# Self-attention on one Trainium2 core: projections and output product on unpadded heads, moved to and from 32-row places through DRAM, and a branch that waits for the mask alone

## The chip, the cores and the metric

The kernel runs on one core of one Trainium2 chip. The metric is the device time of one execution in microseconds (us), given as the median of several runs. A profile is one execution recorded by the hardware. Its engines are TensorE (PE; its weight loads are PEld), VectorE (DVE), ScalarE (ACT), GpSimd (POOL) and SyncE (SP). Each takes its instructions from a queue of its own, in order. SyncE, ScalarE and GpSimd also issue DMAs from their queues; when a DMA has landed, it raises a semaphore, and an instruction that needs the data waits for it on its own engine's queue.

## The reference, cut to what matters

The input x is 8 x 512 x 256 (batches, places, channels), with a side input for attention biases, a condition and a mask of padded places. Two residual steps follow each other, each of two blocks:

```python
x = x + attn(cond(x, bias, mask, cond_64))   # masked attention with a null key, then attention over the heads of a place
x = x + ffn(cond2(x, cond_64))               # a mixture of 8 experts (two per token) and shared ones, then the layer below
```

`ffn` is a transformer layer, and its self-attention is what most of the change touches:

```python
qkv = x @ wi.T + bi
q, k, v = jnp.split(qkv, 3, axis=-1)          # 16 heads of 16 channels each
scores = jnp.einsum('bhqd,bhkd->bhqk', q, k) / jnp.sqrt(hd)
attn = jax.nn.softmax(scores, axis=-1)
o = jnp.einsum('bhqk,bhkd->bhqd', attn, v)
x = layernorm(x + o @ wo.T + bo)
x = layernorm(x + hier_moe(x))                # 8 experts, one per token
```

Only where a key of the mask allows it does `cond` attend to that key; a key is kept where the mask is true, and queries see keys up to their own place and the null key.

## The kernel before, in words

Everything is 32-bit float. P = 128 partitions, S = 512 places in NT = 4 tiles, D = 256 channels in KD = 2 halves, B = 8 batches, H = 16 heads of HD = 16 channels.

**Head and branch.** For this mask no key among the first 384 places is kept in any batch. The kernel tests that: two loads of the mask to one partition, two reductions (L363 to L368), and a value read into registers (L1111) for a branch (L1112) that every engine takes. `any_keys` handles the general case and does not run here; `late_keys` (L812) runs, and attends only from the last 128 queries. Ahead of the branch stand, in queue order, the loads of the constants, of the first attention's weights (wq and wo of 1 MB each, wkv; L370 to L388), of the over-heads attention's weights (`load_oh`, L218), and products with the null key on VectorE (L398, L404). The experts' router and shared weights (L1232 and after) are loaded once the branch is taken.

**Order of the work.** The kernel is one long program, written as Python generators that are advanced by hand. The order in which their calls are recorded, rearranged a little by a scheduler, is the order of each engine's queue. `late_keys` runs together with the routing of the first batches (`route`, `mixture`). From about 388 to 1560 us the self-attention runs in a loop of 256 half steps j, over 32 groups n = j // 8, each of 4 heads of a batch (4 groups a batch). Beside it a plan of side work (routing, experts' matmuls, the next batches' beginnings) is advanced so that it is done by given half steps (`goals`). From 1560 us the last mixture runs.

**Padded heads.** TensorE takes a head's 16 channels as rows that begin at a multiple of 32. So before the change each head has 32 rows, of which 16 hold channels: the projection weights wqp, wkp and the output weights wop are read padded (256 x 512 and 512 x 256), 4 heads fill 128 rows, and the row behind a head's channels holds a one in k and, in q, the negative maximum of a query's scores, so that the second score product gives scores less their maximum.

**One half step** (`half(j)`, h = j % 8) issues, in this order:
- `both` (L1643): two heads' first scores (pss, L1616) for a group ten half steps ahead (8 + LEAD), each reduced to its negative maximum on VectorE (nmz, L1618), and two heads' second scores (pst, L1640) of this group, each passed through exp on ScalarE (pT_s, L1641). pss and pst share four PSUM banks.
- at h = 6, `augment` (L1626): maxima transposed (pm) and added into q_s.
- at h = 1 and 2, `project(n + 2)` (L1561): pq_s (L1568; 4 matmul records a group) evicted by VectorE with bias and scale (L1570), then pk_s (L1574) evicted by ScalarE (L1576). The results q_s and k_s are used where they lie.
- at h = 2 to 5, a step of `divide` (L1676) of the group before; at the end of a batch, `end` (L1696) of the batch before, from the sixth half on.
- side work, and at h = 2, 4, 6 and 7 `gather` (po_s, L1663), four heads' products of weights and values over one tile of keys. v has a column of ones, so that the row behind a head's 16 output rows holds its sums.

**Quotient and output product.** `divide` copies po_s to oT_s on ScalarE (L1679), sends the four rows of sums over 128 partitions (8 KB DMA on ScalarE's queue, L1685), takes reciprocals (L1687), sends them back as rows (SyncE, L1688), and two halves later spreads them over the heads' rows with one product by the constant selb (prs, L1692) and multiplies (L1693). `end` multiplies with wop: four matmuls a tile, one for each padded group (px_s, L1703).

Outside the change, but used as a row to compare with: the experts' result leaves through a 256 KB store from ScalarE's queue (`y<-y`, L1453; 48 times).

Of the kernel before, what the change touches and what calls it, by code (L numbers as in the profile page):

```python
# [9 lines left out]
F32 = mybir.dt.float32  # L10
# [11 lines left out]
H = 16  # L22
# [18 lines left out]
def tile_adaln_attn_ffn(ctx: ExitStack, tc: tile.TileContext, a: dict, out: bass.AP):  # L41
# [29 lines left out]
    cst = keep.tile([P, 270], F32, name="cst", tag="cst")  # L71
    nc.sync.dma_start(cst, a["c_misc"])
    selb = cst[:, 0:128]
    rank8, rank4, rank2 = cst[:, 256:264], cst[:, 264:268], cst[:, 268:270]
# [39 lines left out]
    with nc.allow_non_contiguous_dma(reason="narrow rows"):  # L114
        nc.sync.dma_start(w_chosen, a["w_route"].rearrange("(k p) n -> p k n", p=P))
    br_bc = mid.tile([P, 12], F32, name="br_bc", tag="br_bc")
    nc.scalar.dma_start(br_bc, rows_of(a["b_route"]))
# [77 lines left out]
    none = ohp.tile([P, places // P], I32, name="none", tag="prod", bufs=4)  # L195
    nc.gpsimd.memset(none, B * S)
    nc.sync.dma_start(ids_d.rearrange("(p n) o -> p (n o)", p=P), none)
# [8 lines left out]
    def oh_load(name, shape, src, eng=None):  # L206
        t = ohp.tile(shape, F32, name=name, tag=name)
        (eng or nc.sync).dma_start(t, src)
        return t

    def oh_wload(name, src, cols):
        n = src.shape[0] // P
        return oh_load(name, [P, n, cols], src.rearrange("(k p) n -> p k n", p=P))

    OH_STEPS = 29
    oh_w = {}

    def load_oh():  # L218
        with nc.allow_non_contiguous_dma(reason="small vectors by partition"):
            oh_w["gout"] = oh_load("gout", [P, KD], cols_of(a["g_out"]), nc.scalar)  # L220
            oh_w["bdown"] = oh_load("bdown", [64, 1], a["bdown"].unsqueeze(1), nc.scalar)
        oh_w["awq"] = oh_wload("awq", a["aWq"], D)
        oh_w["awd"] = oh_wload("awd", a["aWdown"], 64)
        oh_w["awup"] = oh_load("awup", [64, 512], a["aWup"])
        oh_w["awout"] = oh_wload("awout", a["aWout"], D)
        oh_w["bq"] = oh_load("bq_bc", [P, D], rows_of(a["bq"]), nc.scalar)
        oh_w["bup"] = oh_load("bup_bc", [P, 2 * D], rows_of(a["bup"]), nc.scalar)
        oh_w["bout"] = oh_load("bout_bc", [P, D], rows_of(a["bout"]), nc.scalar)
# [134 lines left out]
    kept_i = aw.tile([1, 3], I32, name="kept", tag="kept")  # L363
    for u in range(2):
        early_keys = ohp.tile([1, B // 2, LAST * P], U8, name="early_keys", tag="prod", bufs=4)
        nc.sync.dma_start(early_keys, a["mask"][u * (B // 2) : (u + 1) * (B // 2), 0 : LAST * P].unsqueeze(0))
        nc.vector.tensor_reduce(kept_i[:, u : u + 1], early_keys, AX.XY, ALU.max)
    nc.vector.tensor_tensor(kept_i[:, 2:3], kept_i[:, 0:1], kept_i[:, 1:2], ALU.max)  # L368

    def load(name, shape, src, eng=None):  # L370
        t = aw.tile(shape, F32, name=name, tag=name)
        (eng or nc.sync).dma_start(t, src)
        return t

    def wload(name, src, cols):
        n = src.shape[0] // P
        return load(name, [P, n, cols], src.rearrange("(k p) n -> p k n", p=P))

    with nc.allow_non_contiguous_dma(reason="small vectors by partition"):
        gin = load("gin", [P, KD], cols_of(a["g_in"]), nc.scalar)  # L380
        nvcol = aw.tile([P, 1], F32, name="nvcol", tag="nvcol")
        for j in range(2):
            nc.scalar.dma_start(nvcol[j * 64 : (j + 1) * 64, :], a["cond"][1].unsqueeze(1))
    wq = wload("wq", a["Wq"], H * DH)
    wo = wload("wo", a["Wo"], D)
    wkv = wload("wkv", a["Wkv"], 2 * DH)
    nk_bc = load("nk_bc", [P, DH], rows_of(a["cond"][0]), nc.scalar)
    nv_bc = load("nv_bc", [P, DH], rows_of(a["cond"][1]), nc.scalar)  # L388
    nb_bc = load("nb_bc", [P, H], rows_of(a["null_bias"]), nc.scalar)
    load_oh()  # L390
    bias_v = a["attn_bias"].rearrange("(g hh j) q k -> g j q hh k", g=2, hh=4, j=2)


    wn = aw.tile([P, KD, 2, 2, 4], F32, name="wn", tag="wn")
    for k in range(KD):
        for g in range(2):
            pr = ohp.tile([P, 8, DH], F32, name="wn_pr", tag="prod", bufs=4)
            nc.vector.tensor_tensor(  # L398
                pr,
                wq[:, k, g * 512 : (g + 1) * 512].rearrange("p (h d) -> p h d", h=8),  # L400
                bc(nk_bc, 1, 8),
                ALU.mult,
            )
            nc.vector.tensor_reduce(  # L404
                wn[:, k, g].rearrange("p j hh -> p hh j"),
                pr.rearrange("p (hh j) d -> p hh j d", j=2),
                AX.X,
                ALU.add,
            )
# [8 lines left out]
    def any_keys():  # L418
        fill()
# [392 lines left out]
    def late_keys(first_group):  # L812
# [3 lines left out]
        with ExitStack() as ph:  # L816
# [14 lines left out]
            load_x(0)  # L831
            load_x(1)
# [5 lines left out]
            for g in range(2):  # L838
                for j in range(2):
                    nc.sync.dma_start(bias[:, g, j], bias_v[g, j, tail, :, tail])  # L840
                    nc.gpsimd.affine_select(
                        out=bias[:, g, j],
                        in_=bias[:, g, j],
                        pattern=[[0, 4], [-1, P]],
                        compare_op=ALU.is_ge,
                        fill=MASKED,
                        base=0,
                        channel_multiplier=1,
                    )
            ones = wp.tile([1, P], F32, name="ones", tag="ones")  # L850
# [6 lines left out]


            nvb = wp.tile([P, P], F32, name="nvb", tag="nvb")
            nc.vector.tensor_copy(nvb, nvcol.to_broadcast([P, P]))  # L860
            pn = ps_m.tile([P, D], F32, name="pn", tag="m")
            for c in range(8):
                nc.tensor.matmul(pn, nvb, wo[:, c, :], start=(c == 0), stop=(c == 7))
            null_row = wp.tile([1, D], F32, name="null_row", tag="null_row")
            nc.scalar.copy(null_row, pn[0:1, :])
            mv, rs = ln_stats(wk, [pn])
            row = wp.tile([P, D], F32, name="row", tag="row")
            nc.vector.tensor_scalar(row, pn, mv[:, 0, 0:1], rs[:, 0:1], ALU.subtract, ALU.mult)
# [212 lines left out]
            for _ in range(6):  # L1081
                next(prep)

# [27 lines left out]
    kept = nc.values_load(kept_i[:, 2:3], min_val=0, max_val=1)  # L1111
# [110 lines left out]
    with ExitStack() as ph:  # L1222
# [16 lines left out]
        with nc.allow_non_contiguous_dma(reason="small vectors by partition"):  # L1239
            wtT = wload("wtT", a["wtT"], E)  # L1240
            wgT = load("wgT", [64, E], a["wgT"], nc.scalar)
            gT = load("gT", [64, B], a["condT"], nc.scalar)
        swg = wload("swg", a["sw_gate"], 2 * P)
        swu = wload("swu", a["sw_up"], 2 * P)
        swd = wload("swd", a["sw_down"], D)
# [266 lines left out]
        late_keys(chain(route(0), route(1), mixture(0), mixed(0)))  # L1512
# [7 lines left out]
        with nc.allow_non_contiguous_dma(reason="small vectors by partition"):  # L1520
            bqp = load("bqp", [P, 4], cols_of(a["bq_pad"]), nc.scalar)
            bkp = load("bkp", [P, 4], cols_of(a["bk_pad"]), nc.scalar)
        wqp = wload("wqp", a["wq_pad"], 512)
        wkp = wload("wkp", a["wk_pad"], 512)
        wv = wp.tile([P, KD, H, HD], F32, name="wv", tag="wv")
        bv_bc = wp.tile([P, H, HD], F32, name="bv_bc", tag="bv_bc")
        with nc.allow_non_contiguous_dma(reason="values without their padding"):
            for k in range(KD):
                nc.sync.dma_start(
                    wv[:, k], a["wv_pad"][k * P : (k + 1) * P, :].rearrange("p (h d) -> p h d", h=H)[:, :, 0:HD]  # L1530
                )
# [3 lines left out]
        wop = wload("wop", a["wo_pad"], D)  # L1535
# [4 lines left out]
        for t_ in v_sets:  # L1540
# [7 lines left out]
        kone = wp.tile([P, 1], F32, name="kone", tag="kone")  # L1548
        nc.vector.tensor_reduce(
            kone, selb.rearrange("p (h r) -> p h r", h=4)[:, :, 0], AX.X, ALU.add  # L1550
        )
        nc.vector.tensor_tensor(bkp, bkp, kone.to_broadcast([P, 4]), ALU.add)
# [8 lines left out]
        def project(n):  # L1561

            b, g = divmod(n, 4)
# [3 lines left out]
            for k in range(KD):  # L1567
                nc.tensor.matmul(pq, wqp[:, k, gs], yT[:, k, :], start=(k == 0), stop=(k == KD - 1))  # L1568
            q = qs[n] = wk.tile([P, S], F32, name="q_s", tag="q_s", bufs=3)
            nc.vector.tensor_scalar(q, pq, bqp[:, g : g + 1], HD**-0.5, ALU.add, ALU.mult)  # L1570
            yield
            pk = ps_m.tile([P, S], F32, name="pk_s", tag="m")
            for k in range(KD):
                nc.tensor.matmul(pk, wkp[:, k, gs], yT[:, k, :], start=(k == 0), stop=(k == KD - 1))  # L1574
# [498 lines left out]
```

## Time and profile before

| what | value |
|---|---|
| median of 6 runs | 1818.4 us (1815.45 to 1832.13) |
| profiled execution | 1812.23 us |
| its span | 1810.4 us |
| mean granted TensorE clock | 0.902 |
| instructions in the span | 23,454 |
| loop, 405 to 1560 us: TensorE, VectorE, ScalarE, GpSimd busy | 1062.1, 662.5, 411.2, 253.3 us |
| loop: mean share of the DMA engines | 0.23 |

In the profile's busy line an engine's name is followed by its busy time, its share of the span and its number of instructions. A group's row gives the line, the engine, the operation, output and inputs with partitions x elements, and the count; then busy time and mean ns of one; then the idle time just before those instructions, with what ended most of it (`<-DVE nmz L1618` means that VectorE's work at line 1618 ended the wait). A row of the timeline gives start and length in us, then the engine, the line and the operation, with the idle time before it in brackets. The chain is the work that ended last, followed back from the end of the span: each share is what an engine or line holds of it. "DMA share" is the mean busy share of the core's 16 DMA engines. The granted clock is TensorE's, as a fraction of full speed.

The loop's DMA traffic is uneven: from 565 to 660, 860 to 960 and 1165 to 1250 us, where experts' weights stream in, the share is 0.54, 0.67 and 0.61; from 1300 to 1420 us it is 0.03.

### The profile page before, as it was taken

What the parts mean: (1) busy time and instruction counts of PE and PEld (TensorE: products, weight loads), DVE (VectorE), ACT (ScalarE), POOL (GpSimd) and SP (SyncE); (2) the same over time, 40 slices, a digit from 0 to 9 for tenths busy, and PEclk for the clock granted to TensorE, in tenths of its full rate; (3) what the DMA queues carried; (4) which work ended last, traced back from release to release, by engine and by line L of the source; (5) the groups of instructions that cost most, each with busy time, mean ns of one, the idle gap of its engine ahead of it and who ended that gap; (6) DMA issues with size and microseconds to landing.
All of it is one profiled execution on the core that took longest, in us unless ns stands there. A gap on an engine that the chain in (4) does not pass through costs nothing.

```text
span 1810.4 us, 23454 instructions
## 1 busy us (share of the span) xinstructions
PE 1556.4 (86%) x7720; PEld 875.2 (48%) x7720; DVE 1019.3 (56%) x2709; ACT 584.1 (32%) x1281; POOL 561.0 (31%) x534
## 2 busy tenths in 40 slices
PE   2797887888987999998899999899999889639995
PEld 1664655643433553344454444455433333338884
DVE  3867663346655665556445666544746656216556
ACT  0443333202223432333353333344333343213331
POOL 2445343234444434103001301201301001147775
PEclk9897787977878998989899998999999999859998
DMA  5021225920124610002850101472100000047872
GB/s 170 17 101 38 88 84 166 254 71 6 33 68 152 201 59 27 19 1 94 178 174 30 37 7 55 97 199 79 37 1 7 14 1 14 4 162 218 243 217 64
DMA packets 189461, 157.79 MB, mean 87 GB/s; under 512 B 43214, under 2 KB 173774, under 8 KB 189329
## 3 DMA queue, kind: packets, MB, share of 16 engines
q1 hardware_dynamic: 147520, 109.10, 21.7%
q0 software_dynamic: 13056, 29.67, 5.2%
q10 hardware_dynamic: 28752, 17.41, 3.2%
q8 instruction: 64, 1.05, 0.3%
q14 instruction: 69, 0.56, 0.1%
HBM read 117.00 MB, written 44.21 MB: 89 GB/s over the span
## 4 chain that ended last, share of the span: by engine, by line
PE 56%; issue 14%; DVE 14%; POOL 7%; DMA 5%; ACT 1%; SPq 0%; POOLq 0%; DVEq 0%; ACTq 0%
PE pss L1616 13%; PE po_s L1663 6%; PE pg L1436 5%; PE pq_s L1568 3%; PE pk_s L1574 3%; POOL xs L1390 2%; DVE nmz L1618 2%; PE py L1449 2%; PE px_s L1703 2%; POOL pr L321 2%; PE pst L1640 2%; PE pg L1486 2%; PE pu L1493 1%; PE pd L1269 1%; PE prs L1692 1%
## 5 line engine op out<-in xcount | busy, mean ns | idle before, releaser
L1618 DVE TENSOR_REDUCE nmz<-pss 128x1 f32<-128x512 f32 x512 | 334.3, 685 | 224.9 <-PE pst L1640 202.9
L1641 ACT ACTIVATE pT_s<-pst 128x512 f32<-128x512 f32 x512 | 282.9, 595 | 479.6 <-PE pst L1640 464.6
L1616 PE MATMUL pss<-k_s,q_s 32*128 32x512 f32 x1024 | 371.6, 691 | 55.0 <-DVE nmz L1618 54.5
L1640 PE MATMUL pst<-q_s,k_s 32*128 32x512 f32 x1024 | 353.1, 683 | 3.6 <-DVE nmz L1618 2.7
L1616 PEld LDWEIGHTS pss<-k_s,q_s 32*128 32x128 f32 x1024 | 106.0, 194 | 248.3 <-DVE nmz L1618 122.4
L1663 PE MATMUL po_s<-pT_s,v 128*32 128x512 f32 x1024 | 161.7, 637 | 8.7 <-ACT pT_s L1641 8.6
L1278 POOL DMA_INDIRECT yg<-y,slot x64 | 65.4, 1022 | 317.5 <-DMA y<-y 179.3
L321 POOL TENSOR_TENSOR pr<-qk 128x512 f32<-128x512 f32 x72 | 90.2, 1282 | 123.5 <-DVE qk L299 88.4
L321 POOL TENSOR_TENSOR pr<-at,v_h 128x512 f32<-128x512 f32 x72 | 90.7, 1288 | 92.2 <-DVE at L336 61.1
L1436 PE MATMUL pg<-xT,w_gu 128*128 128x128 f32 x768 | 102.4, 288 | 13.8 <-ACT xT L1427 8.4
L1436 PEld LDWEIGHTS pg<-xT,w_gu 128*128 128x128 f32 x768 | 94.3, 198 | 39.3 <-ACT xT L1427 17.2
L1640 PEld LDWEIGHTS pst<-q_s,k_s 32*128 32x128 f32 x1024 | 99.6, 192 | 17.7 <-issue 8.7
L1390 POOL DMA_INDIRECT xs<-x,slot x64 | 63.6, 993 | 140.7 <-DVE slot L1381 121.5
L1907 PE MATMUL py<-w,h_e 128*128 128x256 f32 x368 | 83.5, 379 | 1.3 <-issue 1.3
L1893 PE MATMUL ph<-xTj,w 128*128 128x256 f32 x368 | 84.5, 383 | 0.0
L1896 ACT ACTIVATE h_e<-ph,b 128x256 f32<-128x256 f32 x92 | 43.5, 473 | 107.8 <-PE ph L1893 104.3
L1893 PEld LDWEIGHTS ph<-xTj,w 128*128 128x128 f32 x368 | 70.8, 193 | 9.8
L1211 POOL DMA_INDIRECT ids<-token_id,pi x32 | 31.9, 996 | 135.9 <-DVE pi L1208 119.7
L1907 PEld LDWEIGHTS py<-w,h_e 128*128 128x128 f32 x368 | 68.2, 190 | 10.0 <-issue 1.7
L1441 DVE TENSOR_TENSOR hh<-hh,pg 128x256 f32<-128x256 f32 x48 | 19.9, 416 | 91.1 <-ACT hh L1440 90.9
L1568 PE MATMUL pq_s<-yT,wqp 128*128 128x512 f32 x128 | 65.6, 636 | 0.6 <-DVE hh L1442 0.6
L1574 PE MATMUL pk_s<-yT,wkp 128*128 128x512 f32 x128 | 63.2, 616 | 0.0
(298 smaller groups left out, 2528.8 us busy)
## 6 DMA issues: line engine op xcount, KB each, us to landing
w<-in_w_dram SPq DMA_DIRECT2D x46, 512.0 KB
w_gu<-in_w_gate_dram SPq DMA_DIRECT2D x96, 128.0 KB
w_gu<-in_w_up_dram SPq DMA_DIRECT2D x96, 128.0 KB
w_dn<-in_w_down_dram SPq DMA_DIRECT2D x96, 128.0 KB
xg<-xs SPq DMA_DIRECT2D x48, 256.0 KB
y<-y ACTq DMA_DIRECT2D x48, 256.0 KB
rows<-xr SPq DMA_DIRECT2D x8, 544.0 KB
x<-x SPq DMA_DIRECT2D x8, 512.0 KB
```

Of the source, the lines that this page charges most:

```text
L321: nc.gpsimd.tensor_tensor(pr, x, y, ALU.mult)
L1390: sc_ = nc.gpsimd.indirect_dma_start(out=xs_d, out_offset=bass.IndirectOffsetOnAxis(ap=slot[:, bl, c, t : t + 1], axis=0), in_=xb[bl][:, t ...
L1436: nc.tensor.matmul(pg[:, c, u, :], w[:, u, c, k, :], xT[:, k, u, :], start=(k == 0), stop=(k == KD - 1))
L1568: nc.tensor.matmul(pq, wqp[:, k, gs], yT[:, k, :], start=(k == 0), stop=(k == KD - 1))
L1574: nc.tensor.matmul(pk, wkp[:, k, gs], yT[:, k, :], start=(k == 0), stop=(k == KD - 1))
L1616: nc.tensor.matmul(pss, qs[n][r, t * P : (t + 1) * P], ks[n][r, :], start=True, stop=True)
L1618: yield lambda: nc.vector.tensor_reduce(nmz[n % 2].rearrange("p t (h r) -> p t h r", h=4)[:, t, h, HD : HD + 1], pss, AX.X, ALU.max, negat ...
L1640: nc.tensor.matmul(pst, ks[n][r, c * P : (c + 1) * P], qs[n][r, :], start=True, stop=True)
L1641: yield lambda: nc.scalar.activation(pT[:, u, :], pst, AF.Exp)
L1663: nc.tensor.matmul(pos[n][hd * 32 : hd * 32 + 32, :], v_sets[b % 3][:, c, (4 * g + hd) * VW : (4 * g + hd) * VW + 32], ws[hd // 2][:, hd % ...
L1893: nc.tensor.matmul(ph_, w1[:, k, c * P : (c + 1) * P], xT[:, k, :], start=(k == 0), stop=(k == KD - 1))
L1907: nc.tensor.matmul(py[:, u, :], h[:, c, u * P : (u + 1) * P], w2[:, c, :], start=(c == 0), stop=(c == 3))
```

## The change

**Self-attention.** Weights are loaded padded and compacted on chip (wv and wq by VectorE, wk by ScalarE), so a projection's 128 columns are 8 heads. One `project` serves two groups (n even, halves 0, 1 and 3 of 16). Its q is evicted by ScalarE to q_c, stored to DRAM into 32-row places (rows behind the channels were filled once with zeros for q and a one and zeros for k), and loaded back as a pair of padded groups; k alike. `divide` copies a group's padded output, stores it to DRAM and loads its 64 channel rows back into half of an oT_s that two groups share; reciprocals, rr, prs and the product are done once for two groups. `end` has two matmuls a tile.

```diff
 def project(n):
-            b, g = divmod(n, 4)
+            b, g, u = n // 4, n % 4 // 2, n // 2 % 2
...
-                nc.tensor.matmul(pq, wqp[:, k, gs], yT[:, k, :], start=(k == 0), stop=(k == KD - 1))
-            q = qs[n] = wk.tile([P, S], F32, name="q_s", tag="q_s", bufs=3)
-            nc.vector.tensor_scalar(q, pq, bqp[:, g : g + 1], HD**-0.5, ALU.add, ALU.mult)
+                nc.tensor.matmul(pq, wq_s[:, k, gs], yT[:, k, :], start=(k == 0), stop=(k == KD - 1))
+            qc = wk.tile([P, S], F32, name="q_c", tag="q_c", bufs=1)
+            nc.scalar.activation(qc, pq, AF.Identity, bias=bq[:, g : g + 1], scale=HD**-0.5)
+            nc.scalar.dma_start(own(apart_d[0][u]), qc)
             yield
...
-            kk = ks[n] = wk.tile([P, S], F32, name="k_s", tag="k_s", bufs=3)
-            nc.scalar.activation(kk, pk, AF.Identity, bias=bkp[:, g : g + 1])
+            kc = wk.tile([P, S], F32, name="k_c", tag="k_c", bufs=1)
+            nc.scalar.activation(kc, pk, AF.Identity, bias=bk[:, g : g + 1])
+            nc.scalar.dma_start(own(apart_d[1][u]), kc)
+            yield
+            for w, made in ((0, qs), (1, ks)):
+                pair = wk.tile([P, 2, S], F32, name="qk"[w] + "_s", tag="qk"[w] + "_s")
+                nc.scalar.dma_start(pair, apart_d[w][u].rearrange("(u p) q -> p u q", p=P))
+                for v in range(2):
+                    made[n + v] = pair[:, v, :]
             yield
 def divide(n):
-            oT = oTs[n] = wk.tile([P, S], F32, name="oT_s", tag="oT_s", bufs=5)
-            nc.scalar.copy(oT, pos.pop(n))
...
-            nc.scalar.dma_start(sm, spread(row(oT)))
+            u = n % 2
+            raw = wk.tile([P, S], F32, name="o_s", tag="o_s")
+            nc.scalar.copy(raw, pos.pop(n))
...
+            nc.scalar.dma_start(sm[half_], spread(row))
+            nc.scalar.dma_start(o_d[n % 4], raw)
             yield
+            nc.scalar.dma_start(oT[half_], own(o_d[n % 4]))
+            if u == 0:
+                return
             nc.vector.reciprocal(sm, sm)
-            nc.sync.dma_start(spread(row(rr)), sm)
+            rr = wk.tile([8, S], F32, name="rr", tag="rr")
+            nc.sync.dma_start(spread(rr), sm)
...
-            nc.tensor.matmul(prs, selb, rr, start=True, stop=True)
+            nc.tensor.matmul(prs, sel16, rr, start=True, stop=True)
 def end(b):
-                for g in range(4):
+                for g in range(2):
...
-                        px, oTs[4 * b + g][:, t * P : (t + 1) * P], wop[:, g, :], start=(g == 0), stop=(g == 3)
+                        px, oTs[4 * b + 2 * g][:, t * P : (t + 1) * P], wo_s[:, g, :], start=(g == 0), stop=(g == 1)
...
+        PROJ = (0, 1, 3)
-        for _ in chain(begin(0), project(0), project(1)):
+        for _ in chain(begin(0), project(0)):
...
-            if j % 8 in (1, 2):
-                if j % 8 == 1:
+            if j % 16 in PROJ:
+                if j % 16 == PROJ[0]:
```

`own(t)` is the view of 32-row places that takes the first 16 rows of each. In the built program the scheduler has put each load of q and k close behind its store on ScalarE's queue, with none or one exp or copy between, and each load of oT_s two exps behind its store.

**Head.** The mask's first 384 columns are loaded with the batches on 8 partitions and reduced there; a matmul of 8 values by ones and a minimum with 1 give the branch's value. All loads of weights, and the null key's products, move behind the branch; small constants (w_route, 14 columns of cst, br_bc) stay ahead of it in the built order.

```diff
-    kept_i = aw.tile([1, 3], I32, name="kept", tag="kept")
-    for u in range(2):
-        early_keys = ohp.tile([1, B // 2, LAST * P], U8, name="early_keys", tag="prod", bufs=4)
-        nc.sync.dma_start(early_keys, a["mask"][u * (B // 2) : (u + 1) * (B // 2), 0 : LAST * P].unsqueeze(0))
-        nc.vector.tensor_reduce(kept_i[:, u : u + 1], early_keys, AX.XY, ALU.max)
-    nc.vector.tensor_tensor(kept_i[:, 2:3], kept_i[:, 0:1], kept_i[:, 1:2], ALU.max)
+    early = ohp.tile([B, LAST * P], U8, name="early_keys", tag="prod", bufs=4)
+    nc.sync.dma_start(early, a["mask"][:, 0 : LAST * P])
+    some = ohp.tile([B, 2], F32, name="some", tag="hm")
+    nc.vector.memset(some[:, 1:2], 1.0)
+    nc.vector.tensor_reduce(some[:, 0:1], early, AX.X, ALU.max)
+    kept_i = aw.tile([1, 1], I32, name="kept", tag="kept")
...
+        nc.tensor.matmul(pn, some[:, 0:1], some[:, 1:2], start=True, stop=True)
+        nc.vector.tensor_scalar(kept_i, pn, 1.0, None, ALU.min)
...
             load_x(0)
+            load_weights()
             load_x(1)
...
+            load_oh()
+            load_rest()
+            tables()
```

ScalarE's queue then holds 14 small loads ahead of its first copy in the branch; SyncE's holds the first load of x, then wkv, wq and wo, then the second load of x and the biases.

## The prediction

> **What bounds the kernel now.** I read the busy table and the chain of the page first, then the rows that the change touches, then a quiet stretch of the self-attention loop on TensorE, then the head. From the page:
>
> ```profile
> PE 1556.4 (86%) x7720; PEld 875.2 (48%) x7720; DVE 1019.3 (56%) x2709; ACT 584.1 (32%) x1281; POOL 561.0 (31%) x534
> ...
> PE pss L1616 13%; PE po_s L1663 6%; PE pg L1436 5%; PE pq_s L1568 3%; PE pk_s L1574 3%; POOL xs L1390 2%; DVE nmz L1618 2%; PE py L1449 2%; PE px_s L1703 2%; POOL pr L321 2%; PE pst L1640 2%; PE pg L1486 2%; PE pu L1493 1%; PE pd L1269 1%; PE prs L1692 1%
> ```
>
> TensorE is busy 86% of the span, and in the loop (405 to 1560 us) 1062 of 1155 us, 92%; ScalarE there 411 us, 36%. The four matmul groups that the change halves stand in the chain with 3 + 3 + 2 + 1 = 9%. Their rows, the groups by line:
>
> ```profile
> L1568 PE MATMUL pq_s<-yT,wqp 128*128 128x512 f32 x128 | 65.6, 636 | 0.6 <-DVE hh L1442 0.6
> L1574 PE MATMUL pk_s<-yT,wkp 128*128 128x512 f32 x128 | 63.2, 616 | 0.0
> L1703 PE MATMUL px_s<-wop,oT_s 128*128 128x256 f32 x256 | 62.9, 391 | 0.0
> L1692 PE MATMUL prs<-rr,cst 128*128 128x512 f32 x64 | 40.3, 714 | 5.7 <-DMA rr<-sums 5.7
> ```
>
> None but prs waits for anything: they are pure TensorE time. A stretch without side work, the TensorE timeline from 1361 us (start, length, what, idle before it), shows how the loop ticks:
>
> ```profile
> 1361.71 0.69 PE L1616 MATMUL pss<-k_s,q_s 32*128 32x512 f32 x1 [0.76 <-DVE nmz L1618]
> ...
> 1363.37 1.98 PE L1568 MATMUL pq_s<-yT,wqp 128*128 128x512 f32 x4
> ...
> 1366.35 1.98 PE L1574 MATMUL pk_s<-yT,wkp 128*128 128x512 f32 x4
> 1368.27 1.06 PE L1663 MATMUL po_s<-pT_s,v 128*32 128x512 f32 x8
> ```
>
> A half step's four score matmuls take 1.1 us. Where a half holds nothing else, TensorE then waits 0.76 us for VectorE's two maxima (685 ns each); where it holds pq_s, pk_s, po_s or prs, the wait is covered. So emptied halves pay back part of what they lose.
>
> **Part 1, TensorE's relief.** Two groups of four heads (a pair) now share one pq_s, one pk_s and one prs, and a batch needs half of its px_s matmuls. Half of the busy rows is (65.6 + 63.2 + 62.9 + 40.3) / 2 = 116 us. Half of the 9% chain share is 0.045 x 1810 = 81 us. I stepped a quiet pair through by hand. Now it takes 2 x 23.5 = 47.1 us (one group runs from 1345.73 to 1369.26). After, the built program's order puts pq_s into half 0 and pk_s into half 1 of the even group: it shrinks to about 22.1, since half 0's wait is now covered; the odd group, with three empty halves in a row at 1.9 each, takes about 19.5. That saves 5.4 a pair, 87 over 16 pairs, and px_s up to 31 more: 118, so the 116 is within reach if every stretch behaved so. But most of the loop runs at 36 us a group, with side work in other orders, where the trace's chain gives the four groups only their 9%. I take **-85**, close to the chain's end because that is what ended last; bounds -45 (rival B) and -116. VectorE loses q's eviction (24.0 us) and half of the final products (11 us). I cost that at nothing, as TensorE covers it; VectorE's waits at TensorE stay.
>
> **Part 2, what ScalarE takes on.** Evictions cancel: 32 of k (22.0 us) become 16 of k and 16 of q. New are DMA issues on ScalarE's queue: a pair adds a store and a load for q, the same for k, and a store and a load for each group's output, 8 in all. The nearest row is the experts' 256 KB store on the same queue, 0.38 us an issue: 8 x 16 x 0.38 = 49 us. New too are waits. The built order puts each q or k load behind its store with at most one exp (0.59 us) or copy between, and each output load behind its store with two exps between. A load reads what the store wrote, so ScalarE stops until the store lands, and the exps behind it stop too, whose readers are pst's banks and po_s. The trace has no such wait behind a ScalarE issue; the nearest rows are two 256 KB stores in the chain:
>
> ```profile
> 349.27 6.59 DMA y<-y
> 355.93 0.59 ACT y L1451
> 356.55 2.49 DMA y<-y
> ```
>
> An uncrowded store lands 2.49 us after its issue began. Less 0.38 of issue and 0.6 of exp, a q or k load waits 1.5; less another 0.6, an output load waits 0.9: 2 x 1.5 + 2 x 0.9 = 4.8 a pair, 77 over the loop. With the issues that is **126 us of ScalarE time**. With the 6.59 landing a pair would wait 21; the stretches with a DMA share over 0.5 (565 to 660, 860 to 960, 1165 to 1250, about 280 of 1155 us, 4 of 16 pairs) could cost that, 142 + 49 = 191 in all.
>
> How much of it reaches TensorE? In the quiet stretch ScalarE idles 0.6 to 2.4 us between two pairs of exps. A q event (0.38 + 1.5 + 0.38) in a half with about 1.1 idle shows 1.2; a k event, beside 2.4 idle, 0.4; the output events with 0.6 idle show 0.85 each: 3.3 a quiet pair, 13 for four. In the twelve pairs with side work TensorE has other matmuls ahead, and I take about a third, 1.2 each: 15. Sum **+28**; bounds +10 (0.6 a pair) and +126 (all of it).
>
> **Part 3, the start of the loop.** Today pss starts at 387.78, straight behind two projections of 1.72 + 1.72 us each. After, one projection goes (-3.4), but the first pss waits for evictions, stores, landing and two loads of 512 KB: 0.7 + 2.5 + 0.4 + about 3.5 = 7.1. **+4**, bounds +2 and +12 (a crowded landing). The three padded weights, their compaction and the constant rows have some 25 us between 349 and 375; if that cover is gone, the upper bound pays.
>
> **Part 4, the head.** Now the mask is read by two reductions on one partition, behind 2 MB of weights:
>
> ```profile
> 15.94 3.40 DVE L367 TENSOR_REDUCE kept<-early_keys 1x1 int32<-1x1536 uint8 x2 [5.72 <-DMA early_keys<-in_mask_dram]
> ```
>
> kept is ready at 20.0, GpSimd starts in the branch at 25.1, SyncE and ScalarE at 26.55, and the first xT copy on ScalarE is at 42.50. After, the mask is SyncE's first transfer (issued at 0.8; a 1.9 us landing as sums has from 1561.14 to 1563.03, up to the 5 us of the mask now); 384 columns reduce in about a quarter of 1.7 us, and a tiny matmul and a minimum follow: kept at about 5, the body at about 11. But ScalarE then has 14 small loads to issue (0.50, 0.76 and 1.23 us in its rows there; some 10 us) and a 1.28 us table load before xT: xT at 26 to 28 instead of 42.5. **-15**; bounds -9 (2 MB of weights now stand ahead of the bias and x, whose waits of 4.59 and 5.70 stay) and -20 (those waits shrink).
>
> **Sum.** 1812.2 (profiled execution; span 1810.4) - 85 + 28 + 4 - 15 = 1744. The median of the runs stands 6.2 above the profiled execution, so I forecast **1750**.
>
> [...] The stretch from 1151 to 1526, where the 0.76 us waits are, ran at a granted clock of 0.99, so short waits kept the clock. [...]
>
> **Rivals.**
> A, as forecast: 1720 to 1780.
> B, VectorE takes over: emptied halves only expose its 0.76 us wait, and the relief is about half, 45: 1812 - 45 + 28 + 4 - 15 + 6 = **1790**. For it: pss waits 53.8 us for nmz in the loop already. Against: ten of those 54 us are one wait of 11.3, and the step-through above includes this wait.
> C, slower: the loads' waits stand in ScalarE's one queue ahead of the exps, and all 126 us reach TensorE: 1812 - 85 + 126 + 4 - 15 + 6 = **1848**. It decides once more than 96 of the 126 us show (85 + 15 - 4), or with half of it where landings are like 6.59. For it: at 1358 po_s waits 0.71 us for an exp even today. Against: ScalarE is 36% busy in the loop, and pst's wait for ScalarE is under 1 us in all.
> D, everything hidden: -116 + 10 + 2 - 20: **1694**. For it: TensorE runs at 94 of 95 us in a mixture's stretch, where removed matmuls pay in full.
> That the matmuls do not go is no rival: the built program has half of them.
>
> **How the numbers follow.** A 0.53, B 0.16, C 0.18, D 0.13. About 0.5% (9 us) is what a measurement of this kernel can tell from no change. Faster: A, D, and most of B, 0.77; same 0.05, from B's upper edge and C's lower; slower 0.18. The range goes from D's 1694 up to 1835, into C: it leaves out under 0.1 of C, and a little of D.
>
> **What would show it.** pq_s and pk_s x64, px_s x128, prs x32 with means as now. ScalarE's new issues near 0.38 us, and idle before the q, k and oT loads near 1.5 and 0.9 us; 3 us or more speaks for C. po_s and pss waiting for pT_s by some 28 us instead of 9; if pss waits for nmz by 40 us more, B. First body work at about 11 us and xT near 27. I would be wrong if landings of these stores are far over 2.5 us, or if the loads' issues themselves cost more than 0.4.

## The result, and the profile after

The changed kernel takes **1909.8 us** (median of 20 runs, 1895.2 to 1919.4); the kernel before took 1821.0 in the same comparison. The ratio is 1.0482, with a 95% interval of 1.046 to 1.0503: slower, where 1750 was forecast. In the table of experiments below a median is that of all runs of a kernel and a ratio that of its fast ones alone; one run in four of the late loads (the profiled one) and of the last stores over 16 was slow, over 1.5% above the fastest of the same kernel. The profiled execution's span is 1910.5 us. In lines of the changed kernel, pss is L1679, its maximum nmz L1681, pst L1703, the exp L1704, the stores of q and k L1626 and L1633, their loads L1637, the output's store and load L1748 and L1750.

The page of after, busy time and the chain by line:

```profile
PE 1570.1 (82%) x7434; PEld 876.9 (46%) x7434; DVE 983.8 (51%) x2651; ACT 582.6 (30%) x1283; POOL 562.8 (29%) x533
...
PE pss L1679 11%; PE po_s L1726 5%; DMA k_d<-k_c 5%; PE pg L1468 4%; DMA q_d<-q_c 4%; PE pst L1703 3%; POOL xs L1422 2%; DVE nmz L1681 2%; PE py L1481 2%; DMA o_d<-o_s 2%; POOL pr L325 2%; PE pd L1301 1%; PE pv_s L1658 1%; PE px_s L1770 1%; POOL xg L1951 1%
```

The landings of q's and k's stores now hold 9% of the chain. TensorE is busier than before (1570 against 1556 us), though four of its groups shrank. Those groups, by line:

```profile
L1770 PE MATMUL px_s<-wo_s,oT_s 128*128 128x256 f32 x128 | 39.7, 441 | 1.4 <-DVE oT_s L1760 1.4
...
L1623 PE MATMUL pq_s<-yT,wq_s 128*128 128x512 f32 x64 | 34.5, 665 | 0.0
...
L1630 PE MATMUL pk_s<-yT,wk_s 128*128 128x512 f32 x64 | 31.6, 616 | 0.5 <-DVE hh L1474 0.4
...
L1759 PE MATMUL prs<-rr,sel 8*128 8x512 f32 x32 | 24.5, 854 | 5.0 <-DMA rr<-sums 5.0
```

The counts halved, but three of the four means grew (px_s from 391 to 441 ns). A reason stands in the stretch table for the loop, first of before, then of after (start and end; length; busy time of TensorE, weight loads, VectorE, ScalarE, GpSimd; granted clock; DMA share; GB/s):

```profile
405.00:1560.00 1155.00, 1062.11 (x5434) 496.15 (x5434) 662.50 (x1566) 411.22 (x767) 253.25 (x230) 0.92 0.23 62
```

```profile
405.00:1660.00 1255.00, 1078.31 (x5192) 497.61 (x5192) 634.92 (x1515) 408.61 (x767) 255.27 (x230) 0.85 0.31 86
```

The clock is the third number from the end: 0.92, then 0.85. From the first pss to the last copy of po_s the loop took 1172.8 us before and 1264.4 after. TensorE was idle for 94 and 178 us of that, and at half clock for 188 and 391 us (added up from the trace's clock record). So 92 of the 100 us between the two spans lie in the loop, as idle time and as slower matmuls; the other 9 come before its first pss. What ScalarE waited for in the loop of after (total, times, longest):

```profile
ACT pT_s L1704 <- DMA k_d<-k_c: 88.2, 12, 15.8
...
ACT pT_s L1704 <- DMA q_d<-q_c: 62.5, 11, 14.3
...
ACT pT_s L1704 <- DMA sums<-o_s: 28.4, 24, 1.6
...
ACT hh L1472 <- DMA o_d<-o_s: 10.6, 3, 3.7
```

Exps stood 150.7 us behind loads that waited for a store of q or k, 6.6 us at a time (23 waits), up to 15.8. The 28.4 us put to sums are mostly the two issues that stand ahead of an exp there, 0.58 us for sums and 0.47 for o_d. How much of it TensorE felt stands in its own waits in the loop, first of before, then of after:

```profile
PE po_s L1663 <- ACT pT_s L1641: 8.6, 12, 0.7
...
PE pst L1640 <- ACT pT_s L1641: 0.8, 1, 0.8
```

```profile
PE pss L1679 <- DVE nmz L1681: 50.8, 41, 8.5
PE pst L1703 <- ACT pT_s L1704: 42.5, 15, 8.5
PE pss L1679 <- ACT pT_s L1704: 38.1, 8, 12.4
...
PE po_s L1726 <- ACT pT_s L1704: 8.4, 12, 0.7
```

TensorE waited 89 us for exps, where it had waited 10; for the maxima (nmz) 50.8 us, against 54.5 before. How one such wait acts, first ScalarE's timeline in a fairly quiet stretch:

```profile
1445.15 0.63 ACTq L1626 DMA_DIRECT2D q_d<-q_c  x1
1445.83 0.60 ACT L1704 ACTIVATE pT_s<-pst 128x512 f32<-128x512 f32 x1 [0.70 <-ACT q_c L1625]
1449.72 0.37 ACTq L1637 DMA_DIRECT2D q_s<-q_d  x1
1450.14 0.60 ACT L1704 ACTIVATE pT_s<-pst 128x512 f32<-128x512 f32 x1 [3.71 <-DMA q_d<-q_c]
```

and TensorE's at the same time:

```profile
1447.01 0.59 PE L1703 MATMUL pst<-q_s,k_s 32*128 32x512 f32 x1
...
1450.79 2.07 PE L1703 MATMUL pst<-q_s,k_s 32*128 32x512 f32 x2 [3.18 <-ACT pT_s L1704]
...
1454.65 1.22 PE L1679 MATMUL pss<-k_s,q_s 32*128 32x512 f32 x1
```

The store went out at 1445.15 and the load could only be issued at 1449.72. The exp behind the load had its input long before; pst waited 3.18 us for a bank that this exp had to empty. And from then on the same matmul takes 1.22 us instead of 0.59 to 0.69: the clock record shows half clock from 1450.12 on, for 20.5 us. It fell while TensorE still stood, 2.5 us after its last matmul.

### The profile page after: what moved, and what is told of

Same layout as the page of the kernel before. It is cut to its first block, busy times and chain, and to the rows that moved or that the text cites. A ratio compares the mean times of both kernels' runs of the same rounds, so it can differ in the third digit from the quotient of the medians.

```text
span 1910.5 us, 23012 instructions
## 1 busy us (share of the span) xinstructions
PE 1570.1 (82%) x7434; PEld 876.9 (46%) x7434; DVE 983.8 (51%) x2651; ACT 582.6 (30%) x1283; POOL 562.8 (29%) x533
## 4 chain that ended last, share of the span: by engine, by line
PE 45%; issue 14%; DVE 14%; DMA 14%; POOL 7%; ACT 3%; ACTq 1%; SPq 0%; POOLq 0%; DVEq 0%
PE pss L1679 11%; PE po_s L1726 5%; DMA k_d<-k_c 5%; PE pg L1468 4%; DMA q_d<-q_c 4%; PE pst L1703 3%; POOL xs L1422 2%; DVE nmz L1681 2%; PE py L1481 2%; DMA o_d<-o_s 2%; POOL pr L325 2%; PE pd L1301 1%; PE pv_s L1658 1%; PE px_s L1770 1%; POOL xg L1951 1%
## 5 line engine op out<-in xcount | busy, mean ns | idle before, releaser
L1681 DVE TENSOR_REDUCE nmz<-pss 128x1 f32<-128x512 f32 x512 | 335.4, 685 | 340.0 <-PE pst L1703 188.7
L1679 PE MATMUL pss<-k_s,q_s 32*128 32x512 f32 x1024 | 418.2, 749 | 98.8 <-DVE nmz L1681 50.8
L1704 ACT ACTIVATE pT_s<-pst 128x512 f32<-128x512 f32 x512 | 283.8, 595 | 619.1 <-PE pst L1703 391.3
L1703 PE MATMUL pst<-q_s,k_s 32*128 32x512 f32 x1024 | 413.3, 738 | 44.9 <-ACT pT_s L1704 42.5
L1679 PEld LDWEIGHTS pss<-k_s,q_s 32*128 32x128 f32 x1024 | 122.2, 211 | 311.1 <-DVE nmz L1681 125.6
L1726 PE MATMUL po_s<-pT_s,v 128*32 128x512 f32 x1024 | 175.4, 688 | 8.7 <-ACT pT_s L1704 8.4
L1703 PEld LDWEIGHTS pst<-q_s,k_s 32*128 32x128 f32 x1024 | 119.5, 207 | 80.9 <-ACT pT_s L1704 67.0
L1468 PE MATMUL pg<-xT,w_gu 128*128 128x128 f32 x768 | 106.3, 296 | 20.7 <-ACT xT L1459 20.7
L1468 PEld LDWEIGHTS pg<-xT,w_gu 128*128 128x128 f32 x768 | 98.7, 207 | 47.1 <-ACT xT L1459 32.0
L1726 PEld LDWEIGHTS po_s<-pT_s,v 128*32 128x32 f32 x1024 | 25.0, 114 | 81.3 <-issue 45.2
L1046 ACT ACTIVATE s<-s,ngm 128x128 f32<-128x128 f32 x128 | 49.7, 391 | 36.9 <-DVE ngm L1042 29.7
L1782 POOL TENSOR_TENSOR e_rs<-e_ve,mhalf 128x4 f32<-128x4 f32 x8 | 8.9, 1109 | 174.3 <-DVE e_ve L1780 174.2
```

The costliest lines, as they stand in the source:

```text
L1046: nc.scalar.activation(s[:, h, :], s[:, h, :], AF.Exp, bias=f["ngm"][:, j, h : h + 1], accum_out=f["sm"][:, j, h : h + 1],)
L1468: nc.tensor.matmul(pg[:, c, u, :], w[:, u, c, k, :], xT[:, k, u, :], start=(k == 0), stop=(k == KD - 1))
L1679: nc.tensor.matmul(pss, qs[n][r, t * P : (t + 1) * P], ks[n][r, :], start=True, stop=True)
L1681: yield lambda: nc.vector.tensor_reduce(nmz[n % 2].rearrange("p t (h r) -> p t h r", h=4)[:, t, h, HD : HD + 1], pss, AX.X, ALU.max, negat ...
L1703: nc.tensor.matmul(pst, ks[n][r, c * P : (c + 1) * P], qs[n][r, :], start=True, stop=True)
L1704: yield lambda: nc.scalar.activation(pT[:, u, :], pst, AF.Exp)
```

## The experiments

Two theories were set against each other. **Q**: the loss comes from the place of the loads on ScalarE's in-order queue, ahead of exps. **T**: it comes from 39 MB more of DMA traffic (157.8 to 196.4 MB). Later runs price the relief and the parts. Ratios are to the kernel before on the same chip.

| run | median us | ratio | 95% interval |
|---|---|---|---|
| loads on SyncE | 1795.8 | 0.9883 | 0.9849 to 0.9917 |
| loads from constants | 1768.5 | 0.9709 | 0.9689 to 0.9729 |
| loads late, on ScalarE | 1806.8 | 0.9884 | 0.9829 to 0.9938 |
| half of the matmuls, no moves | 1756.7 | 0.9653 | 0.9631 to 0.9675 |
| moves without relief | 1938.8 | 1.0656 | 1.0583 to 1.0728 |
| output part alone | 1802.5 | 0.9897 | 0.9862 to 0.9933 |
| projections alone | 1901.6 | 1.047 | 1.0428 to 1.0511 |
| head alone | 1812.8 | 0.9968 | 0.9939 to 0.9997 |
| stores over 16 | 1885.5 | 1.0375 | 1.0332 to 1.0418 |
| stores over 16, loads on SyncE | 1800.2 | 0.987 | 0.9778 to 0.9961 |
| straight moves, SyncE | 1773.3 | 0.9713 | 0.9678 to 0.9749 |
| straight moves, GpSimd | 1777.0 | 0.9769 | 0.9726 to 0.9813 |

**Loads on SyncE.** Against after:

```diff
-                nc.scalar.dma_start(pair, apart_d[w][u].rearrange("(u p) q -> p u q", p=P))
+                nc.sync.dma_start(pair, apart_d[w][u].rearrange("(u p) q -> p u q", p=P))
```

> The loads of q and k go out on SyncE's queue instead of ScalarE's; stores, sizes and matmuls stay as after. Theory Q (ScalarE's queue: a load waits there for its store to land, the exps behind it wait too, TensorE idles and its clock falls): ScalarE's idle time before the exps for q_d and k_d (150.7 us after) goes to under 15, the clock returns to 0.90 or more, and the time falls below the kernel before, to 1720 to 1790 us. Theory T (traffic: 39 MB more of DMA crowd the engines' DMA rings, all transfers and the weights come late): the same traffic, so within 1.5% of 1910.

One word on one line takes 114 us away. No exp waits for a store of q or k any more. The traffic is the same, so T falls as the main cause. The mean clock of the profiled execution came back to 0.88 only (0.846 in after, 0.902 before), and the time stayed a little above what Q had named; what TensorE waits for in that loop tells why:

```profile
PE pss L1679 <- DVE nmz L1681: 52.4, 39, 9.8
PE pss L1679 <- DMA k_s<-k_d: 39.0, 6, 9.9
PE pst L1703 <- ACT pT_s L1704: 11.1, 5, 5.2
```

The moves themselves are now late in six places: 39.0 us of pss waiting for k_s.

**Loads from constants.** The loads' source becomes two DRAM tensors filled once.

```diff
-                nc.scalar.dma_start(pair, apart_d[w][u].rearrange("(u p) q -> p u q", p=P))
+                nc.scalar.dma_start(pair, still_d[w].rearrange("(u p) q -> p u q", p=P))
...
```

> The loads of q and k stay on ScalarE's queue but read two DRAM tensors that are filled once ahead of the loop, so they wait for no store; the stores still go out. Every score is then computed from constants, so attention weights and the output are not the reference's, and the last mixture may be balanced differently: only the loop's time is read. Theory Q: the loop falls from 1264 us to under 1120 (before: 1172), clock 0.90 or more. Theory T: traffic is unchanged, the loop stays over 1230.

With all transfers still there and only the dependence gone, the loop's last po_s copy comes at 1518.9 us, against 1661.1 after and 1560.5 before. Q's direction holds, its size doesn't: counted from the first pss the loop is 1161 us, not under 1120. The first pss has nothing to wait for and starts 39 us earlier than in after, so that length isn't comparable. But the end isn't as early as Q said either, and TensorE still waits 69.5 us for nmz. The relief itself was in doubt by then.

**Loads late, on ScalarE.** Same queue, same DMAs; only the order differs.

```diff
-                nc.scalar.dma_start(pair, apart_d[w][u].rearrange("(u p) q -> p u q", p=P))
+                pin(nc.scalar.dma_start(pair, apart_d[w][u].rearrange("(u p) q -> p u q", p=P)))
...
-                yield lambda: nc.scalar.activation(pT[:, u, :], pst, AF.Exp)
+                yield lambda: pin(nc.scalar.activation(pT[:, u, :], pst, AF.Exp))
...
-        PROJ = (0, 1, 3)
+        PROJ = (0, 1, 4)
```

> After, with nothing changed but the order on ScalarE's queue: the loads of q and k are recorded at half 4 of 16 and kept, with the exps, in the recorded order, so that 4 to 8 exps stand between a store and its load. Same DMAs, same queue, same matmuls. Theory Q: most stores have landed by then, the idle time before the exps for q_d and k_d falls from 151 us to under 40, and the time to 1780 to 1830. Theory T, or if any load on ScalarE's queue costs so much: still over 1880.

103 us less than after, from the order alone. The exps' waits for the stores of q and k fell from 150.7 to 5.9 us; with ScalarE's other work behind such a load it is 24 us. pss waits 42.5 us for the loads, much as with SyncE. So the queue is not too slow for the work: the loads stood too early in it.

**Half of the matmuls, no moves.** The kernel before, with one of two input halves in pq_s and pk_s, two of four groups in px_s, half of the columns in prs.

```diff
-            for k in range(KD):
-                nc.tensor.matmul(pq, wqp[:, k, gs], yT[:, k, :], start=(k == 0), stop=(k == KD - 1))
+            for k in range(1):
+                nc.tensor.matmul(pq, wqp[:, k, gs], yT[:, k, :], start=True, stop=True)
...
```

> The kernel before, with half of the matmuls of pq_s, pk_s, px_s and prs left out (one of two input halves, two of four groups, half of the columns and of their product) and nothing moved: the relief of TensorE alone. The output lacks those parts. Theory R (the relief is worth what its busy rows say): 1819 - 116 = about 1703, and at least 81 off, under 1740. Theory V (emptied halves uncover the 0.76 us waits for VectorE, and more idle time lowers TensorE's clock): 40 to 60 us off, 1760 to 1780.

The relief alone is worth 66 us, nearer to V. The four groups fell from 232.0 to 135.3 us of busy time, 97 less. In the loop TensorE's half-clock time rose from 188 to 232 us and its idle time from 94 to 115; pss waits 62.5 us for nmz instead of 54.5. Part of the freed time turns into waits, and matmuls at half clock grow with them.

**Moves without relief.** After, with these matmuls issued twice.

```diff
-            for k in range(KD):
-                nc.tensor.matmul(pq, wq_s[:, k, gs], yT[:, k, :], start=(k == 0), stop=(k == KD - 1))
+            for k in range(2 * KD):
+                nc.tensor.matmul(pq, wq_s[:, k % KD, gs], yT[:, k % KD, :], start=(k == 0), stop=(k == 2 * KD - 1))
...
```

> After with pq_s, pk_s, px_s and prs each issued twice, summed into the same bank, so that TensorE has as many of these matmuls as before while all moves, waits and the head stay: the moves without the relief. q, k, quotient and output product come out doubled, so the output is not the reference's. If relief and waits add up (65 us of relief by the halved matmuls of the kernel before): 1910 + 65 = 1960 to 1990. If TensorE would only have idled in that time, since the loads' waits end the loop's steps: 1910 to 1940.

In after the relief is worth only 1938.8 - 1909.8 = 29 us. The expectation's second case holds: what TensorE saves, it mostly loses again. In the loop it idles 142 us here and 178 in after, and runs at half clock for 318 and 391 us. Exps stand 102 us behind the stores of q and k here, 151 in after. From before, moves and head together cost 117 us.

**The parts.** The output part alone keeps projections as before; the projections alone keep quotient, prs and px_s as before; both have the new head. The head alone keeps the whole self-attention.

> Projections stay on padded heads as before, without any move of q and k; the output part (o_d store, half load, one quotient for two groups, two px matmuls a tile) and the head are as after. Theory Q: its loads sit two exps behind the store and hardly wait, so about 39 us of matmul time goes (px 62.9 to 39.7, prs 40.3 to 24.5) and 6 us at the head, 20 to 30 come back: 1780 to 1810, faster than before. Theory T: 16 of the 39 MB remain, so 1840 to 1870.

> Projections on unpadded heads with q and k moved through DRAM as after, and the head as after; quotient, prs and px on padded heads as before, no o_d. Theory Q: all the q and k waits stay and the output part's relief of about 39 us goes, so 1910 to 1950, as slow as after or slower. Theory T: 24 of the 39 MB remain, about 1870 to 1890.

> The head of after with the self-attention of before. In after's trace the first xT copy is 19 us earlier than before, the first score matmul 11 and the last score of the first attention 6. If only what is left at the end of that stage counts: 1810 to 1815. If the 11 us stay: 1806 to 1810. If the rearranged loads disturb the routing beside it: 1820 or more.

The head gives 9.5 us. The output part gives 10 more on top of the head (1802.5 against 1812.8; the intervals just miss each other), a quarter of the 39 us of matmul time that were to go; its loads hardly wait. The projections alone carry the whole loss: 1901.6, a little under Q's range, with 136 us of exps behind the stores of q and k. The two traces move 12 and 26 MB more than before, where T was worked out with 16 and 24; T named 1840 to 1870 and 1870 to 1890, and both runs miss it.

**Stores over 16.** Why do these stores land late at all? From issue to the last of their semaphore updates the trace of after gives 3.96 us at the least for a store of q or k (median 4.6 for q, 5.0 for k), but 2.13 us for o_d's (median 2.2), of the same 256 KB. No such store landed in 3.85 us, as the expectation below has it; the least of any run is 3.94. One goes out as 8 x 16 x 512, the other as 128 x 512. This run changes the order of the compacted weight columns, so that q_c's rows are channel by head, and stores with channels outermost:

```diff
-            nc.scalar.dma_start(own(apart_d[0][u]), qc)
+            nc.scalar.dma_start(own(apart_d[0][u]).rearrange("h r q -> r h q"), qc)
...
```

> After, with the columns of the compacted q and k weights in the order channel, head instead of head, channel, so that the stores of q and k go to the same 32-row places as 16 x 8 x 512 instead of 8 x 16 x 512; same bytes, same queue, same number of matmuls. In the runs so far the 8 x 16 x 512 store lands no sooner than 3.85 us after its issue, the plain 128 x 512 store of o_d at 2.13. If the outermost dimension sets how many DMA engines a store uses: lands at about 2.1 at best, some 1.7 us less in each of 32 waits, 55 us of ScalarE's wait, of which about 0.7 shows: 1860 to 1880. If the 32-row places themselves are slow: landing stays at 3.85 and the time at 1900 to 1920.

The same bytes to the same places land in 2.81 us at best instead of 3.96 (median 3.8 and 3.4 for q and k), and 24 us of the time go, where 30 to 50 were expected. The crowded waits stay: the longest is still 15.9 us.

> The 16 x 8 x 512 stores together with the loads of q and k on SyncE's queue. With loads on SyncE, pss still waited 39 us for the loads; if the stores land 1.7 us earlier, about half of these waits go: 1765 to 1785, faster than with either alone. If the stores' shape doesn't matter: 1796 again.

Together with the loads on SyncE it gave nothing (1800.2; the interval holds that run's 1795.8). pss still waits 32.7 us for k_s. The expectation's second case came, though the stores do land earlier: k's at a median of 3.65 us, 5.89 with the loads on SyncE alone.

**Straight moves.** Each head's 16 rows go from q_c or k_c directly into one of two lasting pairs, without DRAM.

```diff
+        def move(pair, made):
+            for h in range(8):
+                r = h % 4 * 32
+                nc.sync.dma_start(pair[r : r + HD, h // 4, :], made[h * HD : (h + 1) * HD, :])
...
-            nc.scalar.dma_start(own(apart_d[0][u]), qc)
+            move(pairs[0][u], qc)
...
```

> After with q and k moved from the evicted tile straight into the padded pair, one DMA for each of the 8 heads (16 partitions each), on SyncE's queue, into two pairs each of q and k that keep their constant rows; q's row for the maximum is cleared by a small DMA. No DRAM in between, no wait on ScalarE. Output part and head as after. Theory Q: the wait of pss for the loads, 39 us with loads on SyncE, goes as well, so 1750 to 1785. Theory T: 17 DMAs for each pair instead of 4 crowd SyncE's queue and the rings: 1800 or more.

1773.3 us, the fastest version that computes the reference's output: 2.9% under the kernel before. TensorE's waits in its loop:

```profile
PE pss L1683 <- DVE nmz L1685: 58.6, 41, 11.2
PE pg L1468 <- DMA w_gu<-in_w_gate_dram: 16.9, 4, 12.8
PE po_s L1730 <- ACT pT_s L1708: 8.7, 13, 0.7
PE pss L1683 <- DMA k_s<-k_c: 8.7, 3, 6.2
```

Waiting for k_s is down to 8.7 us, from 39.0 with the loads on SyncE; the wait for the experts' weights w_gu is up, from 4.8 us in the kernel before to 16.9.

> The straight moves of q and k (one DMA a head, SBUF to SBUF) from GpSimd's queue instead of SyncE's. With SyncE, TensorE waited 16.9 us for the experts' weights w_gu, which stood behind the moves on SyncE's queue. If that is so, these waits go and the time is 1755 to 1770. If GpSimd's queue, which also holds the mixtures' scatters and about 1 us of work per DMA, is the worse place: 1780 to 1810.

From GpSimd the wait for w_gu falls under 4 us, as said, but pss then waits 35.4 us in places that the trace shows as its own issue. The time, 1777.0 us, lies between the two expected ranges and is no better than from SyncE, within the spread of these runs.

## Why the prediction was wrong, point by point

**What bounds the kernel** was read rightly, and so was the mechanism of rival C: loads that wait on ScalarE's queue ahead of the exps. What failed is its price, and with it the forecast. In the terms of the sum: the moves with the start of the loop were put at 28 + 4 us and cost 126, the relief was put at 85 and gave 29, the head at 15 and gave 9.5.

**Part 2, the landing.** This is the step that failed first. "An uncrowded store lands 2.49 us after its issue began" was taken from a store of 128 rows to plain rows. The new store took 3.96 us at best, 4.6 (q) and 5.0 (k) at the median and up to 16.4. Of the 32 loads 23 held up an exp, 150.7 us in all, of which 9 are the loads' own issues; 32 x 1.5 = 48 was put down. Issues were dearer too: 0.63 us for a store of q or k, 0.47 and 0.56 for the output's store and load, 0.37 for the loads, 16 x (2 x 0.63 + 2 x 0.37 + 2 x 0.47 + 2 x 0.56) = 65 us instead of 49. The output loads' waits were priced about right (20 us, 29 put down). Its own price for crowded landings, 191 us of ScalarE time, was much nearer than the 126 of the sum, but entered neither the sum nor the bounds.

**Part 2, what reaches TensorE.** The second failure. A third of ScalarE's time was to show in pairs with side work, +28 in all. The runs give 117 + 9.5 = about 126 us for the moves without relief, and 103 to 114 us come back by moving the loads. That this is the very 126 of rival C is luck: C took 126 us of ScalarE time, of which the trace has some 220 (65 of issues, 142 and 15 of waits without them). ScalarE's mean share of 36% said nothing here: the four banks hold one half step's score products, so the exp that came 3.71 us late at 1450 stopped TensorE for 3.18 us, however idle ScalarE is on average. And a stop can cost more than itself, as the 20.5 us at half clock behind the wait of 3.18 show.

**The clock.** The sum held nothing for a slower clock: the stretch with the 0.76 us waits had run at 0.99, and none of the waits worked out for uncrowded stores was over 1.5 us. In after half clock began at 1450 within a wait of 3.18 us and lasted 20.5 us, with further waits of 0.48 and 0.76 us in between. Time at half clock doubled in the loop, from 188 to 391 us. The trace's clock record changes in steps of 3.41 us; after's loop has 255 of them at full clock, and 35 of these were followed by half clock. TensorE stood idle throughout in only 3 of the 35; at the median it was busy for 50% of them, and the longest wait that reached into one was under 2 us for 17 and over 3 us for 15. In the 220 after which full clock stayed it was busy for 100% at the median and never for less than 48%, and the 36 steps before a return to full clock were busy for 88% or more. So half clock came after waits under 2 us as well; what decides it was not shown.

**The store's shape.** The run that puts 16 outermost landed its stores in 2.81 us at best instead of 3.96. The traces also record 9 updates of the semaphore for each 8 x 16 x 512 store and 5 for each 4 x 16 x 512 load of an output, but 16 for each 16 x 8 x 512 and 128 x 512 store. The shape is part of the late landing, not of the crowded part: the longest wait for a store was still 15.9 us. By what means the shape acts was not shown.

**Part 1, the relief.** -85 was too much: alone it is 66, in after 29. The bound of -45 to -116 holds only for the first. The step-through of a quiet pair had the nmz waits in it but not the clock, and half of the busy rows is not removed time when the rest gets slower (102 us of rows went, not 116). Rival B, named for this, had the direction but not the cause: alone, the waits for nmz grew by 8 us, not by 40, and in after they didn't grow.

**Part 3, the start.** +4 was put down. From the first projection to the first pss the chain takes 13.2 us (383.42 to 396.62), against 6.9 with the head alone (371.74 to 378.61): 6.3 more, within the bounds. In it stand the two transfers:

```profile
387.61 5.11 DMA k_d<-k_c
...
392.74 3.75 DMA k_s<-k_d
```

The load took what was estimated (3.5), the store twice as long. The first pss comes 18 us later than with the head alone, but 11 to 12 of these are there before the first projection, nearly all at the first attention's last score, a place that varies as much between runs of the same head (Part 4).

**Part 4, the head.** xT came at 23.5 us, as early as forecast and a little more. But 15 was not the gain: the head alone gives 9.5. In after's chain the time goes to

```profile
10.86 8.40 DMA nvcol<-in_cond_dram
...
20.30 7.62 DMA bias<-in_attn_bias_dram
```

and of 19 us at xT, 11 are left at the first score matmul and 6 at the first attention's last score. These two places vary from run to run, though: in the 12 profiles with the new head the first score comes at 33.8 to 40.8 us and the last at 262.4 to 273.1 (the head alone has the earliest last score, after the latest); in the two with the old head they come at 51.4 and 51.9, and at 273.4 and 278.8. So one pair of profiles doesn't tell how much of the lead is lost inside that stage, and where it goes stays open.

**What stays open.** Why crowded stores take up to 16 us was not taken apart: their shape, transfers ahead on the same queue and the weights' stream all stand beside them. And the idle time and the clock were not separated by a run: every experiment that shortened the waits also raised the clock (median of the runs: 0.846 in after, 0.852 with stores over 16, 0.865 with late loads, 0.874 to 0.880 with loads on SyncE, loads from constants or straight moves). How half clock follows from waits is read off the clock record alone.

## What to carry to other kernels

A DMA that reads what another has just written was a wait on its issuing engine here (150.7 us of exps on ScalarE, 216 us on SyncE's own queue); put it on a queue where nothing urgent stands behind it, or late enough that the write has landed, and look in the built order at what the scheduler made of it. Price a store by a row of its own shape (3.96 us at best here, where a row of another had 2.49), and where no row has it, by the longest landing of a crowded stretch (6.59 us before, 16.4 in after). A share of 36% busy does not mean that an engine in the loop can be stopped for 4 us (one exp, 3.71 us late, cost TensorE 3.18): count how many buffers its consumers and producers have.

## What the runs showed of the hardware

- A 256 KB store from ScalarE's queue to DRAM landed in 2.13 us at best as 128 x 512, in 2.81 as 16 x 8 x 512 and in 3.96 as 8 x 16 x 512; its issue took 0.47 us in the first form and 0.63 in the last. The semaphore of the last form had 9 updates, that of the others 16.
- After a wait of 3.18 us TensorE ran at half clock for 20.5 us, the same matmul taking 1.22 us instead of 0.69. Halving four matmul groups and changing nothing else raised its half-clock time from 188 to 232 us.
- In after's loop 35 steps of 3.41 us at full clock were followed by half clock; TensorE was idle throughout in 3 of them, and busy for 50% at the median.
- Eight DMAs of 16 partitions each from SyncE (1.86 us to land at best) took the place of a 256 KB store and a 512 KB load, with no exp held up behind them, and gave the fastest kernel with the reference's output.
